# Holding back later loads in layer 0 of a four-layer gated cross-attention kernel

## The chip, the cores and the metric

The kernel runs on one core of a Trainium2 chip. A core has five engines that run side by side, each through its own list of instructions in order: TensorE (PE, matrix products into PSUM banks; loads of its stationary operand appear as PEld), VectorE (DVE), ScalarE (ACT, also exponentials), GpSimd (POOL) and SyncE (SP, which here only issues DMA transfers). Semaphores make one wait for another. The metric is the device time of one execution in microseconds, the median of several runs. TensorE's clock is granted in full or in half by the chip, depending on how busy the engine was.

## The reference

Eight batches of 256 tokens (2048 rows of 256 numbers) go through four layers. Each layer adds a gated cross-attention to a context of 77 rows per batch, and then a gated feed-forward part. Only layer 0 and the weights of layer 1's feed-forward part matter here:

```
def feature_map(x, fm_w, fm_b):            # per head of 16 numbers, 16 heads
    z = einsum('nshd,ed->nshe', x, fm_w) + fm_b
    return concatenate([exp(z), exp(-z)], axis=-1)
v, k, q = feature_map(ctx), feature_map(ctx), feature_map(layernorm(x))
scores = einsum('nqhd,nkhd->nhqk', q, k) / sqrt(256)
out = einsum('nhql,nlhd->nqhd', softmax(scores), v).reshape(N, S, 512)
x = x + tanh(g_xattn[0]) * (out @ fc_w.T + fc_b)
x = x + tanh(g_ffn[0]) * (layernorm(x) @ sign(weight).T)
...
w_scale = clip(mean(abs(W)), 1e-5)         # layer 1, feed-forward: ternary weights
Wq = clip(round(W / w_scale), -1, 1) * w_scale
```

Layers 1 to 3 follow (single-head attention and a quantised feed-forward part; a top-k attention with a mixture of experts; a post-norm attention with a binary projection). They take the rest of the time and are not touched.

## The kernel before

**Data.** The 2048 rows are cut into four groups of 512 (`X[0]` to `X[3]`, each 128 partitions by 4 tiles by 256 numbers). A group holds two batches, so group g holds batches 2g and 2g+1. The context lies transposed in `ctxT`. All constants and weights are loaded at the start by SyncE in the order of the program: the feature map's matrix and its bias as a column (`rep`), group 0 (`load_x(0)`, line 78), `ctxT`, the gates and the feature bias as a row on all partitions (`fmb_bc`, line 90), two blocks of vectors (`vec`), some columns, the projection `fcT`, groups 1 to 3, and then ten further weights. The raw ternary weights (`raw_f1w1`, `raw_f1w2`, 1 MB each, line 696) are issued from `ternary` and follow behind.

**Layer 0.** `W2` is built on VectorE from `rep` (lines 333 to 338). `keys(h)` makes the key features `kf` of half the batches (matrix product `pk`, line 356; exponential on ScalarE, line 360). `queries(g)` normalises a group: statistics on VectorE (`ln_st`, `ln_mv`, lines 185 and 186), reciprocal deviations on GpSimd (`ln_rs`, lines 188 and 189), the normalised rows `xn` on VectorE (line 200), eight transposes on TensorE (`pt`, line 210), copies to `xT` on ScalarE and VectorE (lines 214 and 216). GpSimd then adds the gated bias `tfb` to the group (line 258), and `pq` (line 393) with an exponential (line 396) makes the query features `qf`.

For a batch b, `weights(b)` makes for each of two tiles of 128 tokens the scores of 16 heads (`sc`, line 407; four PSUM banks, one such tile at a time), their maximum (`mx`, line 415, VectorE), the difference (`pr`, line 417), the exponential (line 421, ScalarE), the sum and its reciprocal (`sm`, lines 423 and 424), and the product with it (line 425, GpSimd). `values(b)` makes the value features (`pv`, line 370; `zv`, line 375, VectorE; `vf`, line 381, ScalarE). `attend(b)` transposes the weights (`pta`, line 442; copy `aT`, line 443), multiplies them with the values (`po`, line 445; copy `oT`, line 450), projects (`py`, line 457) and adds to the group (`x`, line 462). Four other PSUM banks, handed round, serve all of these but `sc`.

The program's order is: `keys(0)`, `queries(0)`, `weights(0)`, `values(0)`, `keys(1)`, and then for each b the weights and values of batch b+1 ahead of `attend(b)`, with `queries` of the next group before each even b+1.

**Beside layer 0.** A generator, `between`, is advanced after each batch: it calls `ternary` twice (sum of absolute values `w_tot`, line 698; a TensorE product `pm` for the total over partitions, line 700; three passes over the weights, lines 705 to 708, VectorE), `bias_rows` (lines 714 to 735, VectorE) and the first half of layer 1's keys (lines 532 to 549). Behind layer 0's function, before it is called, the sign of layer 0's feed-forward weight is taken on VectorE (`neg` and `sgw`, lines 484 and 485), which the feed-forward part after layer 0 needs (line 275).

**What sets the order.** The program's order isn't the order on the engines. The framework schedules each engine's list when the kernel is built, from its own estimate of when operands will be ready; the list is then fixed, and an engine waits at an instruction whose operand is late even when the next one could run. So a load that is estimated to land early draws the work on its data forward in VectorE's list.

Of the kernel before, what the change touches and what calls it, by code (L numbers as in the profile page):

```python
# [9 lines left out]
F32 = mybir.dt.float32  # L10
# [4 lines left out]
ALU = mybir.AluOpType  # L15
# [4 lines left out]
P = 128  # L20
D = 256
KC = D // P
# [3 lines left out]
NK = NB * SK  # L26
# [3 lines left out]
NG = 4  # L30
GT = NT // NG
GN = GT * P
# [23 lines left out]
def flamingo_kernel(ctx: ExitStack, tc: tile.TileContext, io: dict):  # L56
    nc = tc.nc
# [14 lines left out]
    X = []  # L72
# [4 lines left out]
    def load_x(g):  # L77
        nc.sync.dma_start(
            out=X[g], in_=x_d[g * GN : (g + 1) * GN, :].rearrange("(t p) d -> p t d", p=P)
        )  # L80
# [7 lines left out]
    def load_bc(name, n, dtype=F32, pool=const):  # L88
        t = pool.tile([P, n], dtype, name=f"bc_{name}")
        nc.sync.dma_start(out=t, in_=io[name].partition_broadcast(P))  # L90
        return t
# [10 lines left out]
        out=bcol,  # L102
        in_=io["fm_b"].rearrange("(p o) -> p o", o=1).unsqueeze(0).to_broadcast([8, 16, 1]),
    )
    load_x(0)
    ctxT = load("ctxT", [P, KC, NK])
    gates_raw = load_bc("gates", 8)
    fmb_bc = load_bc("fm_b", 16)
    vecs = []
    for i, (pool, lo, hi) in enumerate(((const01, 0, NV01), (const, NV01, NV))):  # L110
        v = pool.tile([P, hi - lo, D], F32, name=f"vec{i}")
# [4 lines left out]
        vecs.append(v)  # L116
    cols = load("cols", [P, NCOL * KC])
    fcT = load("fcT", [P, 4, D], const01)
    for g in range(1, NG):
        load_x(g)  # L120
    w0f = load("w0f", [P, KC, D], const01)
    wq1 = load("wq1", [P, KC, D], const01)
    wk1 = load("wk1", [P, KC, D], const01)
# [47 lines left out]
    class Banks:  # L171
# [4 lines left out]

        def tile(self, shape, dtype, name, tag):
            return self.pool.tile(shape, dtype, name=name, tag=self.name, bufs=self.n)

    def layer_norm(src, dst, eps=EPS, act=False):  # L180

# [164 lines left out]
    def layer0(psc, ps, a0, a0w, between):  # L346

        tfb = gated(a0, V_FCB, gx(0), "tfb")

        kf = a0.tile([P, 4, NK], F32, name="kf")  # L350

        def keys(h):
            for c in range(4):
# [11 lines left out]
        def values(b):  # L365
            for q in range(2):
                r = 64 * q
                pv = ps.tile([P, 2, P], F32, name="pv", tag="ps")
                for c in range(2):
                    nc.tensor.matmul(  # L370
                        pv[:SK, c, :], ctxT[r : r + 64, c, b * SK : (b + 1) * SK], W2[r : r + 64, :],
                        start=True, stop=True,
                    )
                zv = a0w.tile([SK, 2, 4, 32], F32, name="zv")
                nc.vector.tensor_tensor(
                    zv.rearrange("p c j e -> p (c j) e"),
                    pv[:SK].rearrange("p c (j e) -> p (c j) e", e=32),
                    fb2[:SK].rearrange("p s e -> p (s e)").unsqueeze(1).to_broadcast([SK, 8, 32]),
                    ALU.add,
                )  # L380
                nc.scalar.activation(
                    vf[:, b, :, :].rearrange("p (c q) n -> p c q n", q=2)[:, :, q, :],
                    zv.rearrange("p c j e -> p c (j e)"), AF.Exp,
                )
# [14 lines left out]
        def weights(b, qf):  # L399
            pn2 = []  # L400
            for i in range(2):
                t = 2 * (b % 2) + i

                sc = psc.tile([P, 4, 512], F32, name="sc")
                for c in range(4):
                    for j in range(4):
                        nc.tensor.matmul(
                            sc[:, j, c * SK : (c + 1) * SK],
                            qf[32 * j : 32 * j + 32, c, t * P : (t + 1) * P],
                            kf[32 * j : 32 * j + 32, c, b * SK : (b + 1) * SK],  # L410
                            start=True, stop=True,
                        )
                scv = sc[:, :, : 4 * SK].rearrange("p j (c k) -> p j c k", k=SK)
                mx = small.tile([P, 4, 4], F32, name="mx")
                nc.vector.tensor_reduce(mx, scv, AX.X, ALU.max)  # L415
                pr = a0w.tile([P, 4, 4, SK], F32, name="pr", bufs=6)
                nc.vector.tensor_tensor(
                    pr, scv, mx.unsqueeze(3).to_broadcast([P, 4, 4, SK]), ALU.subtract
                )
                prf = pr.rearrange("p j c k -> p (j c k)")  # L420
                nc.scalar.activation(prf, prf, AF.Exp, scale=1.0 / 16.0)
                sm = small.tile([P, 4, 4], F32, name="sm")
                nc.vector.tensor_reduce(sm, pr, AX.X, ALU.add)
                nc.vector.reciprocal(sm, sm)  # L424
                nc.gpsimd.tensor_tensor(  # L425
                    pr, pr, sm.unsqueeze(3).to_broadcast([P, 4, 4, SK]), ALU.mult
                )
                pn2.append(pr)
            return pn2
# [37 lines left out]
        keys(0)  # L467
        qf = queries(0)
        nxt = weights(0, qf)
        values(0)  # L470
        keys(1)
        for b in range(NB):
# [5 lines left out]
                values(b + 1)  # L478
            attend(b, pn2)
            next(between, None)  # L480

    sgw = w0f
    neg = work.tile([P, KC, D], F32, name="neg", tag="xn")
    nc.vector.tensor_scalar(neg, w0f, 0.0, None, ALU.is_lt)
    nc.vector.scalar_tensor_tensor(sgw, w0f, 0.0, neg, ALU.is_gt, ALU.subtract)


    def one_head_steps(ps, wp, g, qT, kT, b0):
# [204 lines left out]
    def ternary(ps, f1, name, shape):  # L693

        raw = f1.tile(shape, F32, name=f"raw_{name}", tag="raw")
        nc.sync.dma_start(out=raw.rearrange("p a b -> p (a b)"), in_=io[name])
        tot = small.tile([P, 1], F32, name="w_tot")
        nc.vector.tensor_reduce(tot, raw, AX.XY, ALU.add, apply_absolute_value=True)
        pm = ps.tile([P, 512], F32, name="pm", tag="ps")
        nc.tensor.matmul(pm[:, :1], ones, tot, start=True, stop=True)  # L700
        ws = const.tile([P, 1], F32, name=f"ws_{name}")
        nc.vector.tensor_scalar(ws, pm[:, :1], 1.0 / (FF * D), EPS, ALU.mult, ALU.max)
        wr = const.tile([P, 1], F32, name=f"wr_{name}")
        nc.vector.reciprocal(wr, ws)
        nc.vector.tensor_scalar(raw, raw, wr, 1.0, ALU.mult, ALU.min)
        nc.vector.tensor_scalar(raw, raw, -1.0, MAGIC, ALU.max, ALU.add)
        q = const01.tile(shape, BF16, name=f"q_{name}")
        nc.vector.tensor_scalar(q, raw, MAGIC, None, ALU.subtract)
        return q, ws, wr
# [4 lines left out]
    def bias_rows(f1):  # L714
        tmp = f1.tile([P, KC, FF], F32, name="fb", tag="raw")
        fb, row = tmp[:9, 0, :], tmp[:9, 1, :]
        nc.sync.dma_start(out=fb, in_=io["f1b1"].partition_broadcast(9))
        of3 = const01.tile([9, 4], F32, name="of3")
        nc.vector.tensor_scalar(of3[:, 2:3], pidxf[:9], 3.0, -3.0, ALU.is_ge, ALU.mult)
        nc.vector.tensor_scalar(of3[:, 3:4], pidxf[:9], 6.0, -3.0, ALU.is_ge, ALU.mult)  # L720
        nc.vector.tensor_add(of3[:, 2:3], of3[:, 2:3], of3[:, 3:4])
        nc.vector.tensor_add(of3[:, 3:4], of3[:, 2:3], pidxf[:9])
        for j in range(3):
            nc.vector.tensor_scalar(of3[:, j : j + 1], of3[:, 3:4], float(j), None, ALU.is_equal)
        tmp2 = f1.tile([P, KC, 2 * FF], BF16, name="part", tag="raw")
        part = tmp2[:9, 0, :FF]
        for j in range(2):
            nc.vector.tensor_copy(part, fb)
            nc.vector.tensor_tensor(fb, fb, part, ALU.subtract)
            if j == 0:  # L730
                nc.vector.tensor_scalar(row, part, of3[:, 0:1], None, ALU.mult)
            else:
                nc.vector.scalar_tensor_tensor(row, part, of3[:, 1:2], row, ALU.mult, ALU.add)

        nc.vector.scalar_tensor_tensor(brow, fb, of3[:, 2:3], row, ALU.mult, ALU.add)

    b1 = early.enter_context(tc.tile_pool(name="b1", bufs=1))
    with tc.tile_pool(name="a0", bufs=1, reuse_waits="tile") as a0, \
            tc.tile_pool(name="a0w", bufs=2, reuse_waits="tile") as a0w, \
            tc.tile_pool(name="a0s", bufs=1, space=PSUM, reuse_waits="tile") as psc, \  # L740
            tc.tile_pool(name="a0p", bufs=4, space=PSUM, reuse_waits="tile") as ps, \
            tc.tile_pool(name="f1", bufs=2, side="right") as f1:
        kv1, tern = [], []

        def between():
            yield
            tern.append(ternary(ps, f1, "f1w1", [P, KC, FF]))
            yield
            tern.append(ternary(ps, f1, "f1w2", [P, NFC, D]))
            yield  # L750
            bias_rows(f1)
            yield
            kv1.extend(keys1(0, ps, b1))
            yield

        layer0(psc, ps, a0, a0w, between())
        (q1, ws1, wr1), (q2, ws2, _) = tern
# [871 lines left out]
```

## Time and profile before

| | |
|---|---|
| median of 3 runs | 1210.58 us (1210.23 to 1216.09) |
| profiled execution, its own time | 1208.41 us |
| its span, first to last instruction | 1206.3 us |
| TensorE busy | 969.5 us, 80% of the span |
| VectorE busy | 652.6 us, 54% |
| ScalarE busy | 519.7 us, 43% |
| GpSimd busy | 360.4 us, 30% |
| mean granted TensorE clock | 0.842 |
| layer 0, first instruction to its last `py` (line 457) | 0 to 207.5 us |
| DMA, first 30 us | nearly full; then under 4 GB/s until some 240 us |

The profile is one execution taken by the hardware profiler. A row of its timeline has the start in microseconds from the span's start, the duration of the merged instructions, the engine, the line, the operation, the tile written and the tile read, their shapes, the number of instructions, and in brackets the idle time of the engine before them and what ended it. A matrix product in float32 shows as two records, so 32 `sc` are 16 products. Line numbers are those of the kernel before. The granted clock is recorded as a share of full speed; before the first record, near 68 us, the table shows 1.00 whatever the clock was.

### The profile page before, as it was taken

The page shows a single profiled execution, that of the slowest core. Times are in us where ns is not written, and L with a number is a line of the kernel's source. Part 1 is how long each engine was busy: PE and PEld are TensorE (multiplying, and loading weights), DVE is VectorE, ACT ScalarE, POOL GpSimd, SP SyncE. Part 2 cuts the span into 40 slices and gives each one's busy share as a digit, 9 for nine tenths or more (in the row PEclk, how much of TensorE's full clock was granted, in tenths as well). Part 3 has the DMA queues.
Part 4 walks back from the last instruction along what each step waited for, and adds up shares of the span by engine and source line. Part 5 has one row for each costly group of instructions (what it writes and reads, how often), then busy time and mean ns, then how long its engine had stood idle before and what let it go on. Part 6 is the DMA issues. An engine that isn't in the chain of part 4 may idle for free.

```text
span 1206.3 us, 17517 instructions
## 1 busy us (share of the span) xinstructions
PE 969.5 (80%) x6264; PEld 729.2 (60%) x6264; DVE 652.6 (54%) x2788; ACT 519.7 (43%) x1046; POOL 360.4 (30%) x373
## 2 busy tenths in 40 slices
PE   3788798869775686858478989999997999998575
PEld 1465565635343353525356768799996879997453
DVE  6766955566775697896876777142004440000553
ACT  2343444134553655556346666432225642222342
POOL 3331223121200400311132223444426643431441
PEclk9997999969755866576658889999998999999596
DMA  8000000030000000000232245578886438883101
GB/s 294 1 1 3 1 1 1 1 140 1 1 1 1 0 1 1 18 1 1 101 144 79 92 168 195 199 268 330 327 318 225 154 122 311 322 325 150 63 1 35
DMA packets 27659, 132.56 MB, mean 110 GB/s; under 512 B 4548, under 2 KB 15532, under 8 KB 21429
## 3 DMA queue, kind: packets, MB, share of 16 engines
q0 software_dynamic: 11040, 108.54, 24.2%
q1 hardware_dynamic: 16533, 22.91, 5.5%
q8 instruction: 49, 0.80, 0.3%
q14 instruction: 37, 0.30, 0.1%
HBM read 117.02 MB, written 14.42 MB: 109 GB/s over the span
## 4 chain that ended last, share of the span: by engine, by line
PE 46%; DVE 21%; ACT 11%; issue 10%; POOL 8%; DMA 3%; SPq 1%; POOLq 0%; ACTq 0%; DVEq 0%
PE pym L907 8%; PE phm L898 7%; PE pta L1022 4%; DVE pr L1273 3%; PE py L457 2%; PE po L1028 2%; DVE m L1266 2%; PE pta L442 1%; PE sc L978 1%; PE py L1520 1%; PE pyf L665 1%; POOL pr L1016 1%; PE py L1037 1%; PE pq L957 1%; DVE mx L415 1%
## 5 line engine op out<-in xcount | busy, mean ns | idle before, releaser
L898 PE MATMUL phm<-xgT,wt 128*128 128x128 f32 x1472 | 181.9, 278 | 0.5 <-issue 0.5
L898 PEld LDWEIGHTS phm<-xgT,wt 128*128 128x128 f32 x1472 | 176.8, 194 | 5.2 <-issue 2.6
L907 PE MATMUL pym<-wt,hT 128*128 128x256 f32 x736 | 177.2, 389 | 2.0 <-ACT hT L902 1.5
L907 PEld LDWEIGHTS pym<-wt,hT 128*128 128x128 f32 x736 | 137.8, 195 | 20.8 <-ACT hT L902 2.7
L1273 DVE MATCH_REPLACE8 pr<-m,pr 128x77 f32<-128x77 f32 x512 | 107.3, 224 | 0.0
L902 ACT ACTIVATE hT<-phm 128x512 f32<-128x512 f32 x92 | 54.8, 598 | 88.1 <-PE phm L898 65.5
L1016 POOL TENSOR_TENSOR pr<-pr,sm 128x1232 f32<-128x1232 f32 x16 | 36.5, 2279 | 173.6 <-DVE sm L1015 101.0
L873 POOL DMA_INDIRECT wt<-in_w,widx x46 | 45.6, 990 | 135.7 <-PE pym L907 104.0
L1435 DVE TENSOR_TENSOR x<-x,yg 128x512 f32<-128x512 f32 x16 | 13.1, 825 | 129.1 <-DMA yg<-ybuf 129.0
L1266 DVE MAX8 m<-pr 128x8 f32<-128x77 f32 x512 | 77.2, 223 | 0.0
L1022 PE MATMUL pta<-ident,pr 128*77 128x128 f32 x256 | 58.3, 370 | 19.5 <-POOL pr L1016 19.5
L998 ACT ACTIVATE pr<-sc,mx 128x77 f32<-128x77 f32 x256 | 61.6, 340 | 24.8 <-DVE mx L993 24.7
L878 POOL DMA_INDIRECT xg<-xbuf,tok x46 | 45.8, 995 | 83.7 <-PE ptm L884 78.5
L978 PE MATMUL sc<-kT,qT 32*128 32x154 f32 x256 | 47.0, 417 | 28.6 <-ACT pr L998 18.1
L425 POOL TENSOR_TENSOR pr<-pr,sm 128x1232 f32<-128x1232 f32 x16 | 36.8, 2298 | 98.1 <-DVE sm L424 40.5
L912 ACT ACTIVATE yo<-pym,gate 128x256 f32<-128x256 f32 x46 | 22.0, 478 | 101.9 <-issue 76.9
L1024 ACT COPY aT<-pta 77x512 f32<-77x512 f32 x64 | 36.7, 581 | 64.2 <-PE pta L1022 62.1
L1022 PEld LDWEIGHTS pta<-ident,pr 128*77 128x77 f32 x256 | 40.5, 201 | 35.2 <-POOL pr L1016 22.6
L443 ACT COPY aT<-pta 77x512 f32<-77x512 f32 x64 | 35.5, 580 | 59.1 <-PE pta L442 58.9
L913 POOL DMA_INDIRECT ybuf<-yo,row x46 | 46.7, 1014 | 43.7 <-ACT yo L912 32.3
L978 PEld LDWEIGHTS sc<-kT,qT 32*128 32x128 f32 x256 | 29.5, 243 | 42.8 <-ACT pr L998 33.7
L442 PE MATMUL pta<-ident,pr 128*77 128x128 f32 x256 | 44.1, 316 | 9.7 <-POOL pr L425 7.6
(337 smaller groups left out, 1973.6 us busy)
## 6 DMA issues: line engine op xcount, KB each, us to landing
ybuf<-zero SPq DMA_DIRECT2D x8, 512.0 KB, 4.7
yg<-ybuf SPq DMA_DIRECT2D x16, 256.0 KB, 4.8
x<-in_x SPq DMA_DIRECT2D x4, 512.0 KB, 10.9
raw_f1w<-in_f1w SPq DMA_DIRECT2D x2, 1024.0 KB, 6.2
xbuf<-xn SPq DMA_DIRECT2D x4, 512.0 KB, 3.4
out<-x SPq DMA_DIRECT2D x8, 256.0 KB, 2.9
vec<-in_vec SPq DMA_DIRECT2D x1, 896.0 KB, 8.7
wt<-in_w,widx POOLq DMA_INDIRECT x46
```

The lines of the kernel that those rows point to most:

```text
L442: nc.tensor.transpose(pt[:SK, j, :], pn2[i][:, j, c, :], ident)
L878: nc.gpsimd.indirect_dma_start(out=xg[:, :], out_offset=None, in_=xbuf[h][:, :], in_offset=bass.IndirectOffsetOnAxis(ap=tok[:, m : m + 1], ...
L898: nc.tensor.matmul(ph[:, i, :], wt[:, kc * FF + fc * P : kc * FF + (fc + 1) * P], xgT[:, kc, :], start=(kc == 0), stop=(kc == KC - 1),)
L902: nc.scalar.activation(hT[:, NFC // 2 * fq : NFC // 2 * (fq + 1), :], ph, AF.Gelu)
L907: nc.tensor.matmul(py, hT[:, fc, :], wt[:, KC * FF + fc * D : KC * FF + (fc + 1) * D], start=(fc == 0), stop=(fc == NFC - 1),)
L913: nc.gpsimd.indirect_dma_start(out=views[m][:, :], out_offset=bass.IndirectOffsetOnAxis(ap=row[:, m : m + 1], axis=0), in_=yo[:, :], in_of ...
L978: nc.tensor.matmul(sc[:, jj, c * 2 * SK : (c + 1) * 2 * SK], qT[32 * j : 32 * j + 32, c, t * P : (t + 1) * P], kT2[32 * j : 32 * j + 32, c ...
L998: nc.scalar.activation(pr[:, j0 + jj, c, :], sc[:, jj, c * SK : (c + 1) * SK], AF.Identity, bias=mx[:, jj, c : c + 1], scale=-1.0,)
L1016: nc.gpsimd.tensor_tensor(pr, pr, sm.unsqueeze(3).to_broadcast([P, 4, 4, SK]), ALU.mult)
L1022: nc.tensor.transpose(pt[:SK, j, :], pr[:, j, 2 * c + q, :], ident)
L1266: nc.vector.max(m8[:, i, :], row)
L1273: nc.vector.match_replace(row, m8[:, i, :], row, -BIG)
```

## The change

Four things are done in layer 0.

1. The feature bias row (`fmb_bc`) and the gates are loaded before group 0 and not after `ctxT`.
2. Groups 1 to 3 are no longer loaded at the start, but inside `layer0`, after the first batch's weights. A new function, `follow`, copies one number on ScalarE from the end of a finished tile into the first element of a destination; the load that overwrites the destination must wait for that copy. Here the source is the last element of group 0's query features `qf`.
3. Each raw ternary weight is loaded behind such a copy from the last element of the key features `kf`.
4. The sign of the feed-forward weight is taken from `between`, after `bias_rows`, in a buffer of the ternary weights' pool, which is seeded in the same way.

```diff
+    fmb_bc = load_bc("fm_b", 16)
+    gates_raw = load_bc("gates", 8)
     load_x(0)
     ctxT = load("ctxT", [P, KC, NK])
-    gates_raw = load_bc("gates", 8)
-    fmb_bc = load_bc("fm_b", 16)
...
     cols = load("cols", [P, NCOL * KC])
     fcT = load("fcT", [P, 4, D], const01)
-    for g in range(1, NG):
-        load_x(g)
     w0f = load("w0f", [P, KC, D], const01)
...
+    def follow(dst, src):
+
+        nc.scalar.copy(dst, src)
...
         kf = a0.tile([P, 4, NK], F32, name="kf")
+        kfs.append(kf)
...
         keys(0)
         qf = queries(0)
         nxt = weights(0, qf)
+        for g in range(1, NG):
+            follow(X[g][0:1, 0, 0:1], qf[0:1, 3, GN - 1 :])
+            load_x(g)
         values(0)
         keys(1)
...
-    sgw = w0f
-    neg = work.tile([P, KC, D], F32, name="neg", tag="xn")
-    nc.vector.tensor_scalar(neg, w0f, 0.0, None, ALU.is_lt)
-    nc.vector.scalar_tensor_tensor(sgw, w0f, 0.0, neg, ALU.is_gt, ALU.subtract)
...
         raw = f1.tile(shape, F32, name=f"raw_{name}", tag="raw")
+        follow(raw[0:1, 0, 0:1], kfs[0][0:1, 3, NK - 1 :])
         nc.sync.dma_start(out=raw.rearrange("p a b -> p (a b)"), in_=io[name])
...
-        kv1, tern = [], []
+        kv1, tern, kfs = [], [], []
...
             bias_rows(f1)
+            neg = f1.tile([P, KC, D], F32, name="neg", tag="raw")
+            follow(neg[0:1, 0, 0:1], kfs[0][0:1, 3, NK - 1 :])
+            nc.vector.tensor_scalar(neg, w0f, 0.0, None, ALU.is_lt)
+            nc.vector.scalar_tensor_tensor(sgw, w0f, 0.0, neg, ALU.is_gt, ALU.subtract)
             yield
```

`sgw = w0f` now stands ahead of the call of `layer0`.

More of the change, by code (lines that the diff above doesn't have):

```diff
@@ L735, in bias_rows @@
         nc.vector.scalar_tensor_tensor(brow, fb, of3[:, 2:3], row, ALU.mult, ALU.add)
+    sgw = w0f
     b1 = early.enter_context(tc.tile_pool(name="b1", bufs=1))
```

## The prediction

> **What bounds the kernel now.** I read the page's engine shares first (TensorE 80% busy, VectorE 54%, DMA a quarter), so no engine is full over the whole span, and a local change must be priced from the waits of its own stage. Then the timeline of the first 130 us, where layer 0 runs.
>
> ```profile
> 7.08 0.75 DVE L185 BATCH_NORM_STATS2 ln_st<-x 128x6 f32<-128x256 f32 x2 [6.04 <-DMA x<-in_x]
> 10.54 0.18 DVE L340 COPY fb<-bc_fm_b 128x16 f32<-128x16 f32 x1 [1.71 <-DMA bc_fm_b<-in_fm_b]
> 16.60 0.75 DVE L185 BATCH_NORM_STATS2 ln_st<-x 128x6 f32<-128x256 f32 x2 [2.51 <-DMA x<-in_x]
> 21.52 0.41 DVE L200 TENSOR_SCALAR xn<-x,ln_mv,ln_rs 128x256 f32<-128x256 f32 x1
> 22.07 0.66 PE L210 MATMUL pt<-ident,xn 128*128 128x128 f32 x2 [6.46 <-DVE xn L200]
> 29.16 2.14 PE L407 MATMUL sc<-kf,qf 32*128 32x77 f32 x32
> 31.42 2.25 DVE L698 TENSOR_REDUCE w_tot<-raw_f1w 128x1 f32<-128x2048 f32 x1
> 33.59 1.43 DVE L415 TENSOR_REDUCE mx<-sc 128x16 f32<-128x1232 f32 x1
> 47.19 2.25 POOL L425 TENSOR_TENSOR pr<-pr,sm 128x1232 f32<-128x1232 f32 x1 [2.09 <-DVE sm L424]
> ...
> 64.53 5.36 PE L457 MATMUL py<-w_fcT,oT 128*128 128x256 f32 x16
> 69.93 0.75 DVE L462 SCALAR_TENSOR_TENSOR x<-py,gates,x 128x512 f32<-128x512 f32 x1 [2.94 <-PE py L457]
> 73.10 2.34 POOL L258 TENSOR_TENSOR x<-x,tfb 128x1024 f32<-128x1024 f32 x1 [3.72 <-DVE xn L200]
> 75.17 1.44 DVE L415 TENSOR_REDUCE mx<-sc 128x16 f32<-128x1232 f32 x1 [1.53 <-PE sc L407]
> 88.14 2.86 PE L457 MATMUL py<-w_fcT,oT 128*128 128x256 f32 x12 [0.20 <-DVE oT L450]
> 93.57 1.43 DVE L415 TENSOR_REDUCE mx<-sc 128x16 f32<-128x1232 f32 x1
> 108.47 5.58 PE L457 MATMUL py<-w_fcT,oT 128*128 128x256 f32 x16
> ```
>
> Columns: start, duration, engine and line, what, count, idle time before it and its releaser. Group 0 has landed at 7.08, but its normalising (L200) runs only at 21.52: VectorE, which works in order, first stands before the statistics of groups 1 to 3 while their rows land. Even when the first scores are there (29.16 + 2.14 = 31.3), their maximum waits till 33.59 behind the sum over a ternary weight (L698).
>
> Then the table by stretch: after the bracket of times the length, busy time of TensorE, its weight loads, VectorE, ScalarE, GpSimd, and the granted clock.
>
> ```profile
> 91.80:95.20 3.40, 1.71 (x20) 1.12 (x20) 3.40 (x4) 1.16 (x2) 0.00 (x0) 1.00 0.05 16
> 95.20:112.30 17.10, 15.76 (x97) 10.43 (x98) 9.83 (x15) 6.47 (x10) 4.71 (x4) 0.50 0.00 0
> 114.00:138.00 24.00, 20.11 (x215) 13.41 (x213) 23.92 (x32) 10.53 (x17) 4.58 (x2) 1.00 0.01 2
> 136.00:153.00 17.00, 13.43 (x145) 9.45 (x146) 15.55 (x23) 7.42 (x12) 7.37 (x5) 1.00 0.00 1
> ```
>
> After 3.4 us with TensorE half idle the clock falls to 0.50 for 17 us; it comes back during a run of `py` (the 16 at 108.47). From 48 to 68 the column's 1.00 is only the lack of a record: 32 `sc` take 2.0 us there and 1.13 later: slow too. In the third line VectorE is the bound (23.92 of 24).
>
> **The change, part by part.** Times are of the profiled execution: span 1206.3, own time 1208.41, 2.2 under the median 1210.58. Batches of layer 0 are b0 to b7; orders come from the built instruction streams.
>
> *Head.* Two small broadcasts now precede group 0's load. Lower bound: two issues of 0.47 each, +0.9. Upper: the two broadcasts landed at 9.30 and 10.54, 1.24 apart, twice that is +2.5. I take +1.4, nearer the issue row: statistics at 8.5, done at 10.3 (1.8, as before). The 1.71 wait for `fm_b` is gone, the bias being first. The small constants (10.63 to 12.43) take 1.8, so `tfb` starts at 12.1, `W2` is done at 13.1 as before (13.14), and the four `xn` (0.33 each) directly behind. `pk` 13.1 to 15.5 (2.42), eight `pt` at 0.26 to 17.5; half way, at 16.6, ScalarE copies `xT` (0.59), then `pq` twice 2.08: first `sc` at 21.4 instead of 29.16, -7.8. Its maximum at 23.5 instead of 33.59, -10.1, since neither `w_tot` nor statistics stand before it. The three tiny copies behind `qf` and the loads behind them: issue at 22.3, landing by 29 (0.5 MB each, 10.9 us when queued, 1.7 apart); VectorE asks for group 1 at 28.6. The raw weights are issued near 31 (6.2 to landing) and asked for at 40.5. On SyncE's queue the ten weight loads move ahead of groups 1 to 3, some 5 us sooner, for users far later; behind the held loads stand only the raw weights and, at 93, a bias row. Cover enough, so 0; with it gone VectorE would stand before `sm`, some 2 us.
> The Trainium skill, DMA: Bandwidth & Descriptors, "Rules for kernel authors", advises issuing a transfer early and waiting late, which speaks against this. The two margins above say it costs nothing here; if the rule bit, the sum would lose those 2 us.
>
> *b0.* From the first maximum to GpSimd's second normalising (47.19) it is 13.6 before. Now the first exponent queues behind the `kf` copies (+1.5), 1.5 us of statistics sit between `pr` and `sm`, and the third maximum goes ahead of the second reciprocal: 15.6, so 39.1, -8.1, its end 41.4. From there to the end of `py` TensorE is the bound, 49.49 to 69.89 = 20.4; group 1's `pt` moves into it, +2.0 at low clock. End 63.8 instead of 69.9, -6.1. Second `w_tot` and group 1's `xn` (4 x 0.33) lie beside, in VectorE's idle 9 us of 16.5.
>
> *Between b0 and b1.* The statistics of groups 2 and 3 now stand behind `x` (L462) and before b1's maximum, and one goes through GpSimd: `x` 0.67; group 2's last three statistics 1.26; its `ln_rs` 1.45; four `xn` 1.37; GpSimd's add of `tfb` (2.34 at 73.10) ahead of group 3's `ln_rs` 1.45; one `xn` 0.33. That is 8.9 from the end of `py`, where it was 5.3 (69.89 to 75.17): maximum at 72.7, -2.5. So 7.6 of the 10.1 us gained are given back here and in b0.
>
> *b1, the clock.* TensorE has its `sc`, `pv` and first eight `pta` done by 69.6 and must wait for `zv` at 74.4, with one `po` (0.64) between. That is less work than in the 3.4 us that lost the clock at 95.2. So b1 runs at half clock: maximum to end of `py` 20.3, by b2's row (93.57 to 113.8), end at 93.0 instead of 91.0. Lower bound: warm, 15.8 (75.17 to 91.0). The ternary chain L705 to L708 (4.75) then ends 1.2 later, not 2.5: next maximum at 94.2, +0.6.
> The Trainium skill, TensorE: Matmul & The Clock Gate, "HAM oscillation — how this bites in real kernels", says to avoid TensorE idle gaps over about 3.4 us. The row at 91.80 lost the clock with 1.71 of 3.4 busy, so without a whole idle gap; by the rule the two gaps here would cost nothing and the sum would be that of the second rival, by the row it is the one below. I go by the row.
>
> *b2.* Before it was the cold batch, 20.3. The last 12 `py` of b1 should bring the clock back, as at 108.47. Warm batches take 13.2 (139.72 to 152.95) to 15.8; I take 14.5, between two that resemble it: end 108.7 instead of 113.8, -5.1. Bounds -6.4 and, still cold, +0.6.
>
> *b3, b4.* `neg` (0.33) and the sign (0.60) come into the stretch where VectorE is full: +0.9. TensorE's order lets a quarter of `py` and three of `pk` into gaps before 149.3, in a stretch that it bounds till 158.5: 0 to -2, I take -0.9. Together 0. The three seed copies (0.2 each) lie in ScalarE's idle time.
>
> Sum -5.1: 1203.3 on the profiled time, 1205.5 against the median.
>
> **The rivals.** 0.5% (6 us) is about what a measurement of this kernel tells from no change.
> - *The forecast*: half clock in b1, full in b2: 1205.5; alone 1202 to 1210.
> - *The clock stays up in b1 as well.* For it: the two gaps are not one whole idle stretch. Against: the row at 91.80. b1 15.8, ends at 88.5 (-2.5); b2 warm, -5.8 more: -8.3, 1202.3.
> - *Other side: the clock isn't back for b2.* Its place is b1's `py`, now 4 and then 12 with other work between, where both recorded returns had 16 in a row; it decides when no clock window holds enough of the 12. Then b2 is 20.3 too: +0.6, and +0.9 from the sign uncovered: +1.5, 1212.1.
> - *A slower one of another kind*: after 235 us the clock toggles in many stretches; the whole tail is moved against them. The unchanged kernel's own runs reach 1216.1, 7.7 above the profiled one. Against -5.1 it must cost over 11 us to be seen as slower: 1217.
> - *That the change does nothing*: VectorE's built order has no statistics of other groups before group 0's `xn` any more, so no.
>
> **How the numbers follow.** Forecast 0.46, clock up in both 0.17, cold in both 0.24, tail 0.13. Faster by over 0.5% means below 1204.5: nearly half of the first, most of the second: 0.21 + 0.15 = 0.36. Slower means above 1216.6: most of the tail and a little of the third: 0.14. The rest, 0.50, is within. The range leaves out about 0.1 on each side: 1200 to 1214.5.
>
> **What would show it.** First `sc` near 21 and its maximum near 23.5 (head); end of b0's `py` near 64; b1's maximum near 73 behind an `xn` that waits for `ln_rs`; granted clock 0.50 between about 74 and 92; b2's `py` ending before 110 with the clock up. The prediction is wrong if b1's maximum comes before 69 (the GpSimd chain isn't as long), if the clock never falls in b1, or if it falls again in b2.

## The result, and the profile after

The changed kernel takes 1209.63 us (median of 22 runs, 1201.64 to 1220.59), the kernel before, run beside it, 1209.80 (22 runs, 1198.90 to 1222.13). The ratio is 1.0007, its 95% interval 0.9984 to 1.0031: -1.9 to +3.8 us, no difference that can be measured. The ratios leave out runs more than 1.5% above the fastest of their kernel, which the medians and means given here keep; without them the gains in the four pairs of shortened kernels compared further down are 6.9, 4.1, -1.4 and 4.0 us in the mean, instead of 6.3, 2.2, 0.9 and 2.8. The profiled execution took 1207.88 us, its span is 1206.1 us (before 1206.3), its mean granted clock 0.827 (before 0.842).

So the total did not move, though the head of the kernel did. The timeline of the changed kernel, its rows for the instructions that the prediction looked at (start, duration, engine and line, what, count, idle time before and its releaser; lines are two to four higher than before):

```profile
10.12 0.75 DVE L187 BATCH_NORM_STATS2 ln_st<-x 128x6 f32<-128x256 f32 x2 [2.94 <-DMA x<-in_x]
21.64 2.18 PE L410 MATMUL sc<-kf,qf 32*128 32x77 f32 x32
23.89 1.44 DVE L418 TENSOR_REDUCE mx<-sc 128x16 f32<-128x1232 f32 x1 [3.48 <-PE sc L410]
38.67 2.25 POOL L428 TENSOR_TENSOR pr<-pr,sm 128x1232 f32<-128x1232 f32 x1 [4.72 <-DVE sm L427]
55.43 2.81 PE L460 MATMUL py<-w_fcT,oT 128*128 128x256 f32 x12
58.28 0.75 DVE L465 SCALAR_TENSOR_TENSOR x<-py,gates,x 128x512 f32<-128x512 f32 x1 [0.16 <-PE py L460]
62.09 1.38 DVE L202 TENSOR_SCALAR xn<-x,ln_mv,ln_rs 128x256 f32<-128x256 f32 x4 [1.16 <-POOL ln_rs L191]
63.55 2.35 POOL L260 TENSOR_TENSOR x<-x,tfb 128x1024 f32<-128x1024 f32 x1 [1.50 <-DVE xn L202]
67.25 0.41 DVE L202 TENSOR_SCALAR xn<-x,ln_mv,ln_rs 128x256 f32<-128x256 f32 x1 [2.20 <-POOL ln_rs L191]
67.58 1.43 DVE L418 TENSOR_REDUCE mx<-sc 128x16 f32<-128x1232 f32 x1
69.40 1.14 PE L445 MATMUL pta<-ident,pr 128*77 128x128 f32 x4 [4.09 <-DVE zv L378]
82.02 2.86 PE L460 MATMUL py<-w_fcT,oT 128*128 128x256 f32 x12 [0.20 <-DVE oT L453]
87.18 1.43 DVE L418 TENSOR_REDUCE mx<-sc 128x16 f32<-128x1232 f32 x1
97.34 3.74 PE L460 MATMUL py<-w_fcT,oT 128*128 128x256 f32 x16
```

What to see: the first scores 7.5 us sooner (21.64, before 29.16), their maximum 9.7 us sooner, the chain from `x` over two `ln_rs` and GpSimd's add to the next maximum (58.28 to 67.58), the wait for `zv` behind it, and `py` of b2 at full clock (16 in 3.74 us, before 5.58, most of it at half clock). In layer 0 no wait of VectorE for a transfer is left after 10.12.

The lead is largest at b2: its last `x` starts at 101.1 (before 114.1, 13.0 us later). Layer 0's last `x` starts at 198.0 (before 207.5: 9.5). At 300 us matched instructions are only 2.0 us sooner, from 450 us on, but for a few, less than 0.3. Layer 0's lead is real in this execution, and gone before half of the span. The granted clock shows where it begins to go. The table of stretches of the changed kernel, cut at the changes of the clock (bracket of times, length, then TensorE, its loads, VectorE, ScalarE, GpSimd, granted clock, DMA share, GB/s):

```profile
228.09:255.39 27.30, 16.64 (x41) 7.30 (x42) 18.63 (x64) 5.87 (x10) 8.42 (x7) 0.50 0.21 84
255.39:265.63 10.24, 7.87 (x56) 4.93 (x54) 3.64 (x10) 6.93 (x10) 0.00 (x0) 1.00 0.47 188
265.63:279.29 13.66, 12.94 (x44) 7.84 (x45) 7.83 (x23) 3.90 (x6) 0.00 (x0) 0.50 0.00 0
279.29:306.59 27.30, 24.19 (x125) 15.34 (x124) 15.60 (x49) 12.00 (x29) 6.29 (x10) 1.00 0.00 1
```

and of the kernel before:

```profile
238.55:262.45 23.90, 13.23 (x36) 5.15 (x35) 17.16 (x57) 5.62 (x9) 8.41 (x7) 0.50 0.18 70
262.45:310.23 47.78, 40.45 (x234) 25.80 (x234) 28.50 (x87) 24.09 (x48) 7.91 (x10) 1.00 0.14 54
```

Both run the same instructions in the same order here; the order differs only in layer 0. The changed kernel has a second half-clock stretch, 265.63 to 279.29, that the other has not. All these lengths are whole multiples of 3.413 us (27.30 is 8 of them, 13.66 is 4, 47.78 is 14): the clock changes on a grid. For nearly the same work (266 and 270 entries on TensorE) the changed kernel needs 23 steps here, the other 21.

### The profile page after: what moved, and what is told of

It reads as the page before. It is cut to its first block, busy times and chain, and to the rows that moved or that the text cites. A ratio compares the mean times of both kernels' runs of the same rounds, so it can differ in the third digit from the quotient of the medians.

```text
span 1206.1 us, 17522 instructions
## 1 busy us (share of the span) xinstructions
PE 968.7 (80%) x6264; PEld 729.7 (60%) x6264; DVE 650.5 (54%) x2788; ACT 520.5 (43%) x1052; POOL 360.7 (30%) x373
## 4 chain that ended last, share of the span: by engine, by line
PE 55%; DVE 20%; ACT 10%; issue 6%; POOL 6%; DMA 1%; SPq 0%; ACTq 0%; POOLq 0%; DVEq 0%
PE pym L914 11%; PE phm L905 11%; PE pta L1029 4%; DVE pr L1280 3%; PE po L1035 2%; PE pta L445 2%; PE py L460 2%; DVE m L1273 2%; PE pyf L666 2%; PE py L1527 1%; PE ph L645 1%; PE sc L985 1%; POOL pr L1023 1%; PE py L1044 1%; PE po L448 1%
## 5 line engine op out<-in xcount | busy, mean ns | idle before, releaser
L1442 DVE TENSOR_TENSOR x<-x,yg 128x512 f32<-128x512 f32 x16 | 13.1, 825 | 129.5 <-DMA yg<-ybuf 129.4
```

## The experiments

As in the prediction, a stage bN ends with `py` and `x` of batch N; the scores taken in it are the next batch's. The first theory: layer 0 really is faster, and layers 1 and 2 give it back through half-clock stretches. Rivals: a later wait of fixed end; luck of the two profiles.

### Cut behind layer 0

```
         layer0(psc, ps, a0, a0w, between())
         (q1, ws1, wr1), (q2, ws2, _) = tern
+    for g in range(NG):
+        nc.sync.dma_start(out=out_d[g * GN : (g + 1) * GN, :]..., in_=X[g])
+    (the rest left out)
```

> The kernel before, cut off behind layer 0's attention: the four groups are written out there, and layer 0's feed-forward and layers 1 to 3 are left out. Layer 0's last x is at 207.5 in the profile, so about 216 with the output. It is the measure for the next run.

> The changed kernel, cut off at the same place. My theory (layer 0 really is shorter, the gain is given back in layers 1 and 2): 9.5 us less than the other cut kernel, as the traces show it (198.0 instead of 207.5). Rival 'luck': the profile of after shows a favourable fall of the clock windows and that of before an unfavourable one, and in the mean of many runs layer 0 gained little: 0 to 3 us less. Rival 'fixed wait' (some later wait ends at a time that layer 0 does not set): 9.5 less here too.

Measured: before 213.62 us (5 runs, 213.07 to 216.24), changed 206.79 (5 runs, 206.50 to 210.35): 6.8 less by the medians, 6.3 by the means, and no run of the one overlaps the other. Luck alone falls; the size is less than the two profiles' 9.5. Leaving out the rest changes the order of some instructions beside layer 0 in both and takes some away (the statistics and normalising of the feed-forward part, 12 VectorE instructions in b3 and b4 alone), so the size need not be that of the whole kernels.

### Cut behind 285 us

> The kernel before, cut off behind layer 1's first two groups of attention and its first group of feed-forward (about 285 us in the profile, about 292 with the output); all that follows is left out. Measure for the next run.

> The changed kernel, cut off at the same place. My theory (the gain is lost between 235 and 285 us to half-clock stretches): 2 us less than the other, with at most half of layer 0's gain left. 'Luck': 0 to 3 us less, the same as after layer 0. 'Fixed wait' behind 285 us: still 9 us less.

The same edit behind `cross1(1, ...)`. Measured: 295.15 us (5 runs, 291.60 to 297.46) and 291.50 (6 runs, 288.61 to 301.09): 3.7 less by the medians, 2.2 by the means, with overlap. A wait of fixed end behind 285 us, which asked for 9 here, is not what takes the gain; part of it seems to have gone by then.

### The tail moved by extra work

```
     def project_tokens(ps, g, xT, w, gate):
+        if g == 0:
+            dm = ps.tile([P, 512], F32, name="dm", tag="ps")
+            for _ in range(15):
+                nc.tensor.matmul(dm, w[:, 0, :P], xT[:, 0, :], start=True, stop=True)
```

> The changed kernel with 15 extra matmuls of 128x512 (0.46 us each at full clock, 6.9 us together; their result is not used) ahead of layer 0's feed-forward, so that all behind layer 0 comes as late as in the kernel before, with TensorE busy meanwhile. 'The tail absorbs a shift' (my theory): the total stays within 3 us of the changed kernel's 1209.6. 'A shift passes through' (layer 0's gain is lost to something else): 1214 to 1218.

TensorE's row of this kernel:

```profile
199.85 13.04 PE L275 MATMUL dm<-xT,w_w0f 128*128 128x512 f32 x30
```

Measured: 1220.65 us (6 runs, 1214.77 to 1229.97), ratio to the kernel before 1.0132 (1.0086 to 1.0179). The 15 matmuls stand as 30 entries of 0.43 us, so the shift is twice what I had reckoned: 13.04 us, with the small order that it changes 13.7. Of these 11 arrive in the total by the medians, 15 by the two ratios to the kernel before. "The tail absorbs a shift" falls: a lost microsecond does pass through, within the scatter. A gained one was not tested here.

But its profile shows something better, again the table of stretches:

```profile
242.36:269.67 27.31, 16.66 (x41) 7.31 (x42) 18.65 (x64) 5.89 (x10) 8.41 (x7) 0.50 0.21 84
269.67:279.91 10.24, 7.86 (x56) 4.93 (x54) 3.63 (x10) 6.92 (x10) 0.00 (x0) 1.00 0.47 187
279.91:293.56 13.65, 12.95 (x44) 7.82 (x45) 7.82 (x23) 3.88 (x6) 0.00 (x0) 0.50 0.00 1
293.56:320.87 27.31, 24.18 (x125) 15.32 (x124) 15.59 (x49) 12.02 (x29) 6.30 (x10) 1.00 0.00 1
```

Line by line it is the changed kernel's table, 14.27 us later. The grid itself lies 0.62 us later in this execution; the rest, 13.65, is four steps. Moved by whole steps, the work meets the same clock, here up to 370 us. Then the two part by 2.3 us: behind a step in which TensorE was busy all 3.41 us in both, the shifted kernel's clock comes back (at 385.7) and the changed one's does not (at 371.5). So the place on the grid does not settle everything.

### The clock held up

```
     def normal1(g, ps, f1w, act):
+        if g == 0:
+            dm = ps.tile([P, 512], F32, name="dm", tag="ps")
+            for _ in range(20):
+                nc.tensor.matmul(dm, ident, wk2..., start=True, stop=True)
     ...                                    # and 5 more ahead of pyf, in ffn1 for n == 1
```

In layer 1's feed-forward part, VectorE scales the rows of a group (`q_r`, small factors for each row), TensorE transposes these (`p`), multiplies (`ph`), and multiplies again (`pyf`) after ScalarE has copied the transposed result to `hiT`; `pq` and `sc` are queries and scores of layer 1's attention. The wait that the extra matmuls are to fill, in the changed kernel:

```profile
242.50 0.59 PE L625 MATMUL p<-identb,q_r 128*9 128x128 bf16 x4 [10.66 <-DVE q_r L620]
```

> The kernel before with 20 extra matmuls of 128x512 in the 10.7 us in which TensorE waits for q_r, and 5 in the 2.5 us in which it waits for hiT behind Gelu's table load: the clock should not fall at 238.55, and the stretches of ph, pq, sc and pyf to 285 us run at full clock. My theory: about 4 us less at 285 us than the kernel before; in the total 0 to 5 less, as far as the tail does not absorb it.

> The same 25 matmuls in the changed kernel. My theory (the gain goes to half-clock stretches between 235 and 285 us): at 290 us it is 6 to 9 us ahead of the other filled kernel instead of 2, and in the total 4 to 9 us. Rival 'later': still ahead by 6 at 290 us, but level in the total, the half-clock stretches behind 300 us doing it. Rival 'luck': 0 to 2 us at both places.

The order of some `ph`, `pq` and `pt` close by changes with it, alike in both. Measured: 1202.96 us (12 runs; ratio to the kernel before 0.9954, 0.9924 to 0.9984) and 1202.11 (12 runs; 0.9967, 0.9938 to 0.9995). Both are faster, but by the same: the 4 to 9 us between them were not found. The profile of the filled changed kernel shows the price and what it buys:

```profile
231.99 18.98 PE L608 MATMUL dm<-w_wk,ident 128*128 128x512 f32 x40
```

```profile
235.30:303.56 68.26, 65.72 (x303) 36.39 (x301) 40.65 (x126) 27.85 (x49) 14.10 (x16) 1.00 0.16 62
```

The extra work fills 19 us where 10.7 were free, and yet the kernel is some 4 us faster than the kernel before by the ratio (0.6 to 7.5): the clock stays at 1.00 for 68 us.

Then 15 matmuls that nearly fit the gaps (11, 2 and 2), in the cut kernels and in the whole changed one:

> The kernel before, cut off at the second place (about 285 us), with 15 extra matmuls of 128x512 (0.9 us each by the last runs, twice what I had reckoned): 11 in the 10.7 us before p, 2 among the scores ahead of it, 2 in the gap before pyf, so that TensorE's clock does not fall there. The filled kernels lost 6.7 us to the surplus of their matmuls and were still 5 us faster; without the surplus this one should take 286 to 289, against 295.2 without the matmuls.

> The changed kernel with the same 15 matmuls, cut off at the same place. If the half-clock stretches between 228 and 285 us are what takes layer 0's gain, it is 5.5 to 7.5 us ahead of its filled counterpart, as at the end of layer 0 (6.8), so 279 to 282. If they only add scatter and the gain is taken elsewhere, it is 2 to 4 us ahead, as without the matmuls (3.7).

> The whole changed kernel with these 15 matmuls. Against 1209.6: by the filled kernels' -5 and their surplus of 6.7 to 9 us, 1195 to 1199. If the tail behind 300 us goes by its own clock stretches and only scatters, the gain passes through in the mean; if a gain ahead of it is always taken back, 1203 to 1207.

Measured: 289.73 (6 runs, 285.03 to 291.58), 288.58 (5 runs, 284.65 to 291.47) and 1201.36 us (12 runs, 1192.43 to 1210.56; ratio 0.9956, 0.9922 to 0.9990). Between the cut kernels lies 1.2 us, where the first theory asked for 5.5 to 7.5: as a statement on the mean it falls, as far as 5 and 6 runs tell. The smaller number of matmuls saved no more than the 25 had. Still, this kernel and the two filled ones are the fastest measured here, and the one with the kernel before inside is as fast as those with the change.

### The place on the grid

As above, with `range(2)`.

> The changed kernel with only 2 extra matmuls (1.7 us; with the little order that they change, the work behind them should come 2.4 us later, as 15 of them moved it by 13.7). In the profiles, the clock changes only on a grid of 3.413 us, and the stretch from 228 to 323 us of the changed kernel came out the same to 0.02 us when it was moved by exactly four such steps. New theory: where the work of layer 1 stands within a step of the grid decides how many half-clock stretches it gets, and the kernel before has a cheaper place than the changed one. 2.4 us put the changed kernel's work on the place that the kernel before had: the second half-clock stretch (265.6 to 279.3) should be gone, the work at 300 us come 4 to 5 us sooner than in the changed kernel although 2.4 us were added, and the total be 1204 to 1209. Rival, the place does not matter: all behind comes 2.4 us later, total 1212.

Measured: 1203.14 us (12 runs, 1197.41 to 1210.63), ratio to the kernel before 0.9983 (0.9950 to 1.0016). The rival asks for 2.4 us more than the changed kernel, a ratio of 1.0027; that lies above the interval, but the changed kernel's own 1.0007 is known only to 0.9984 to 1.0031, so in the mean the rival is unlikely and not excluded. Nor is it shown that this kernel is faster than the changed one in the mean: the two intervals overlap. Its table of stretches:

```profile
237.50:261.40 23.90, 13.25 (x36) 5.17 (x35) 17.14 (x57) 5.62 (x9) 8.40 (x7) 0.50 0.18 69
261.40:309.18 47.78, 40.47 (x234) 25.82 (x234) 28.50 (x87) 24.07 (x48) 7.92 (x10) 1.00 0.14 54
```

It is the table of the kernel before, 1.05 us earlier, down to the counts, and stays so up to 700 us; the grid lies 1.05 us earlier in this execution too. The second half-clock stretch is gone, as expected. "4 to 5 us sooner at 300 us" missed: layer 0 ended 5.9 us later than in the changed kernel's profile (203.9), 2.4 were added, and 300 us came 0.95 later. So that stretch was 7.4 us cheaper. The place is the one aimed at all the same: behind layer 0 the work comes 8.5 us later than in the changed kernel and the grid 0.8 earlier, 9.3 us against the grid; for the kernel before it is 9.5 less 0.2, 9.3 too, two steps and 2.5 us.

### GpSimd's part of the chain

```
-        for g in range(1, NG):
-            follow(X[g][0:1, 0, 0:1], qf[0:1, 3, GN - 1 :])
-            load_x(g)
+        follow(X[1][0:1, 0, 0:1], qf[0:1, 3, GN - 1 :])
+        load_x(1)
     ...
                 nxt = weights(b + 1, qf)
+                if b == 1:
+                    for g in range(2, NG):
+                        follow(X[g][0:1, 0, 0:1], nxt[0][0:1, 3, 3, SK - 1 :])
+                        load_x(g)
```

> The changed kernel cut off behind layer 0's attention, with the loads of groups 2 and 3 held further, behind the second batch pair's weights, so that neither their statistics nor GpSimd's add of tfb stand ahead of the maximum at 67.6 us. If that chain costs what the trace shows (the maximum comes 9.3 us behind the end of py; 4 to 5 us of it are waits for ln_rs and GpSimd), the maximum comes 4 to 6 us sooner and the kernel takes 202 to 204 instead of 206.8. Rival: statistics and ternary work come elsewhere in VectorE's full stretch, and nothing is gained (206 to 208).

VectorE's rows of its timeline:

```profile
58.16 0.75 DVE L465 SCALAR_TENSOR_TENSOR x<-py,gates,x 128x512 f32<-128x512 f32 x1 [1.96 <-PE py L460]
62.22 1.44 DVE L418 TENSOR_REDUCE mx<-sc 128x16 f32<-128x1232 f32 x1 [3.30 <-PE sc L410]
```

The maximum comes 4.1 us behind `x` instead of 9.3 (and 9.6 in the other cut kernel), and in this profile b1 keeps full clock (up from 50.0 to 101.2). Measured: 205.27 us (6 runs, 202.12 to 208.67) against 206.79: 1.5 less by the medians, 2.8 by the means, with overlap. The chain's price is as the trace has it; what it is worth at layer 0's end is less than expected and not sure.

## Why the prediction was right or wrong

Start of a stage's last `x` or length of the stages between them, us, in every profile of a kernel with layer 0 as before, and with it as changed (in the two `cut0` kernels some instructions stand in another order than in the whole kernels):

```
profile             b0 ends  b1    b2    b3+b4  b7 ends  half clock between 110 and 150
before              69.9     23.0  21.2  38.9   207.5    up to 112.3 only (from b2)
cut0_before         69.5     23.0  21.1  39.9   206.6    up to 111.9 only
cut1_before         69.2     23.0  21.1  38.9   206.8    up to 111.5 only
cut1_warm_before    70.2     22.9  19.6  38.9   206.1    up to 110.2 only
fill_before         69.6     22.9  14.7  38.9   200.6    none
after               58.3     28.2  14.6  43.9   198.0    112.0-115.4, 132.5-139.3
cut0_after          61.0     28.3  21.2  40.0   203.5    none
cut1_after          57.5     28.2  14.6  48.8   202.1    111.2-128.3, 141.9-145.3
cut1_warm_after     57.9     28.4  14.6  48.8   202.7    111.9-128.9, 142.6-146.0
shift_after         58.7     28.3  14.6  44.0   198.5    112.7-116.1, 133.1-140.0
fill_after          58.6     28.3  14.6  43.9   198.4    112.4-115.8, 132.9-139.7
warm_after          58.0     29.2  21.2  44.8   206.2    127.6-131.0, 137.8-148.1
nudge_after         57.8     33.6  15.2  44.4   203.9    135.1-145.3
```

*Head.* Statistics at 10.12, 3.0 us later and not 1.4: two small broadcasts ahead of the 0.5 MB cost more than the upper bound of 2.5, and `pk` began at 15.37 and not at 13.1. By luck it was not felt: the clock was up from 19.87 to 30.11, which the forecast did not have, and the 8 entries of `pq` took 2.09 us and not 4.16. First `sc` 21.64 for 21.4, maximum 23.89 for 23.5.

*Held loads.* Costed at nothing, and nothing it was: VectorE waits for none of them. The rule to issue early (the Trainium skill, DMA: Bandwidth & Descriptors, "Rules for kernel authors") was broken here free of charge.

*b0.* GpSimd's second normalising 38.67 for 39.1. The end of `py` 58.2 for 63.8: wrong by 5.6, because I kept half clock to the end of b0; it came back at 50.59, before at 67.89.

*The chain to the next maximum.* 9.3 us from `py`'s end for 8.9, in the order foretold. The maximum itself came at 67.58, not 72.7, and so under the 69 at which I had called the prediction wrong; not for the reason named there (a shorter chain), but because b0 ended sooner.

*b1.* Half clock, as forecast, but for 6.8 us and not for 18:

```profile
67.66:74.49 6.83, 4.88 (x45) 4.36 (x46) 6.83 (x10) 3.01 (x5) 2.35 (x1) 0.50 0.01 2
```

It doesn't decide between the row and the rule of the idle gap, as the forecast had it: the wait for `zv` came in one piece of 4.09 us (the row at 69.40), not as two gaps with the `po` between, and the clock fell 2.35 us into it. It came back behind `sc` and `pta`, without a run of `py`. From end to end b1 takes 28.2 to 28.4 in six of eight profiles, forecast 29.2. Take the chain away and the clock stays up, as the last experiment shows.

*b2.* 14.6 us for 15.7, with the clock up in six of eight; in two it was 21.2, the price of the rival "not back for b2" but not its way: there the clock was back in b1 and fell again 3 us into b2 (at 91.85 and 90.02), which the forecast had named as a sign of being wrong. The reason given for that rival, 16 `py` in a row, was not needed for a return in b1.

*b3, b4: the step that failed.* "Together 0", the sum of +0.9 (sign) and -0.9 (order): the stages take 43.9 to 48.8 in seven of eight profiles, before 38.9 in four of five. The seven have half-clock stretches in them, of 10.2 to 20.5 us together, and lose 0.43 to 0.54 of that time (the profile of the changed kernel 5.0 of 10.2). The one without takes 40.0, against 39.9 of its counterpart: there the sign and the order did come to nothing. What the sum lacked is a term for the clock. VectorE is full here and hands TensorE just enough work. The table of stretches, changed kernel, the two steps that each stand ahead of a loss, and what follows the second:

```profile
108.60:112.03 3.43, 2.14 (x35) 1.43 (x38) 3.43 (x5) 1.79 (x4) 0.00 (x0) 1.00 0.00 0
129.10:132.50 3.40, 1.96 (x40) 1.57 (x44) 3.40 (x8) 2.42 (x4) 0.00 (x0) 1.00 0.00 0
132.50:139.30 6.80, 6.13 (x34) 4.02 (x27) 5.54 (x10) 3.06 (x6) 3.26 (x3) 0.50 0.01 2
```

and the kernel before in its two leanest:

```profile
122.50:125.90 3.40, 2.40 (x42) 2.10 (x43) 3.40 (x6) 2.48 (x4) 0.00 (x0) 1.00 0.00 0
139.60:143.00 3.40, 2.44 (x20) 1.45 (x20) 3.40 (x5) 1.91 (x5) 0.00 (x0) 1.00 0.00 0
```

In these steps TensorE busy for 2.4 of 3.4 us kept the clock, for 2.0 to 2.1 lost it. It is no sharp threshold, as two other steps at full clock show, the first of the kernel before, the second of `fill_before`, in the stage where the kernel before lost the clock with 1.71; full clock followed both:

```profile
272.69:276.10 3.41, 1.91 (x14) 1.63 (x15) 2.77 (x8) 2.29 (x4) 0.00 (x0) 1.00 0.00 0
91.28:94.69 3.41, 1.78 (x16) 1.19 (x16) 3.38 (x5) 1.16 (x2) 0.00 (x0) 1.00 0.06 16
```

Counted over the steps at full clock in the first 330 us of all 14 profiles, the clock fell behind 31 of 31 with TensorE busy under 1.5 us, 24 of 29 with 1.5 to 2.0, 18 of 45 with 2.0 to 2.4, and 2 of 696 with more. The table of stretches before had shown 20.11 of 24 busy there and I took that for safe; a mean over 24 us says little about its leanest 3.4. Whether the moved sign, the order or the new place on the grid makes those steps leaner wasn't separated.

*Sum.* Layer 0 ends 9.5 us sooner in the profile, 6.3 in the mean of the cut kernels, 3.9 in the means of the table (205.5 and 201.7); forecast 5.1. That the profile's size comes near is luck: two errors cancelled, b0 was 5.5 better, b3 and b4 about 5 worse. Apart from the two `cut0` kernels, TensorE runs the same list in layer 0 in all profiles of a group, and still layer 0 ends anywhere between 200.6 and 207.5 (before) and between 198.0 and 206.2 (changed).

*The tail.* The forecast let the rest pass unchanged, hence 1205.5; the measured 1209.63 lies inside its range, but of the 5 us forecast none is left. The rival "the whole tail is moved against them" is nearer: moved by 9.5 us, layer 1 cost two grid steps more (6.8 us), and by 300 us 7.5 us were gone in the profile. I had asked of it over 11 us and 1217; it took about what layer 0 had won. What stays open is the mean: the kernels cut at 285 us are 1 to 4 us apart, the whole ones 0 within 4, layer 0 by 4 to 7; at which place the rest goes on average, these runs don't settle, since each profile is one throw.

The Trainium skill, TensorE: Matmul & The Clock Gate, "HAM oscillation — how this bites in real kernels", asks to avoid idle gaps over about 3.4 us. Here the clock fell behind steps of 3.4 us in which TensorE was busy for 2.0 to 2.1 us, and sometimes stayed behind others with 1.8 to 1.9; the measured steps decide.

## What to carry to other kernels

Where TensorE's clock is granted by steps, price a change in two parts: the work that leaves the path, and every step further on whose load it may thin. Read the leanest 3.4 us of each stage that the engine shares with a full feeder, not the stage's mean; here the clock was at risk behind a step with under 2.4 us busy and was lost behind every one with under 1.5. A local win of a few microseconds in such a kernel must be confirmed by many runs of the whole: one profile of each can show 9.5 us where the total has none, and here a few useless matmuls in a wait were worth more (0.3 to 0.5%) than the change itself (nothing that could be measured).

## What the runs showed of the hardware that was not expected

- Clock changes lie on a grid of 3.413 us. It isn't tied to the program's start: in 14 profiles it lay 0.0 to 3.2 us behind the first instruction, in 11 of them 2.0 to 3.2.
- Work at the same place against that grid met the same clock to 0.02 us over 90 us (moved by four steps; they part at 370 us), or up to 700 us (the nudged kernel and the kernel before). Nearly the same instructions took 71.68 us from one clock loss to another on one place of the grid and 78.50 on another.
- In the changed kernel's 22 runs the span (1199.9 to 1218.8 us) goes with the time at half clock (worked out from each run's span and mean clock), correlation 0.90, 0.32 us per microsecond: most of the scatter between its runs goes with the clock. In the 68 runs of the kernel before that were taken beside the experiments the correlation is only 0.42, so this is shown for the changed kernel alone.
- 25 matmuls whose result nobody reads, some 8 us of them beyond the 10.7 us wait that most of them fill, made both kernels 0.3 to 0.5% faster.
